# Last layer: context values and their sums from one product, the weights turned by transposes; feed-forward columns in fours, 64-row products side by side

## The chip, the core and the metric

The kernel runs on one core of one Trainium2 chip. The metric is the time of one execution on the device, in microseconds. The engines named below are TensorE (PE, with its weight loads shown as PEld), VectorE (DVE), ScalarE (ACT), GpSimd (POOL) and SyncE (SP), which issues most of the DMAs. Products accumulate in PSUM, which the kernel divides into eight banks of 128 x 512 fp32 values.

## What is computed

Four transformer layers over x of 8 batches x 256 tokens x 320 channels, with a context of 8 x 120 rows of 192 channels. Everything is fp32 but the attention of layer 0, which is quantised. In outline:

```python
# layer 0: quantised attention (20 heads of 16)
x = x + attention(ln(x), ln(x), Wq1, Wk1, Wv1, Wo1, bo1, 20)
x = x + attention(ln(x), ctx, Wq2, Wk2, Wv2, Wo2, bo2, 20)
x = x + (a * gelu(g)) @ W2 + b2        # a, g = split(ln(x) @ W1 + b1), 1280 each
# layer 1: the same without quantisation
# layer 2: attention to the first 104 context rows plus attention to the last 16, then Wo
# layer 3 (8 heads of 40): enc = ctx[:, :116], ca = ctx[:, 116:]
hs = mha(x @ Wq, enc @ Wk, enc @ Wv)
ca_q1 = einsum('btc,th->bch', ca, Wq_ca)[:, np.linspace(0, 191, 256).astype(int), :]
ca_hs1 = mha(ca_q1, x, x)
ca_hs2 = mha(ca_hs1 @ Wq, ca @ Wk_ca, ca @ Wv_ca)
out = (hs + ca_hs2) @ Wout + b_out + x
```

The 256 queries `ca_q1` of layer 3 are 192 distinct ones: the index list takes every third one twice.

## The kernel before

**Products.** 320 channels are two tiles of 128 rows and one of 64. So a projection is two "whole-row" products (K = 128) and one 64-row product. Where two outputs are made together, their 64-row operands lie on partitions 0–63 and 64–127, so that the two use different halves of PE's array. `duo` (L122) does this: whole rows of all outputs first, then the 64-row products of all. `by_weight` and `by_token` (L132–L140) list the three terms for weights or tokens as the stationary side. `mm` (L117) is a plain accumulation.

**PSUM.** The pool `ps_f` has three buffers of two banks (`pair()`), the pool `ps_a` two single banks (`bank()`). Whoever asks for a buffer waits until the older user of it has been read.

**Layer 0** is the class `Quant`. `project_all` (L1143) walks the eight batches: v of the batch (one `duo`), the turn of the next batch (`turned`: six transposes and four activations that apply the layer norm's scale and bias), q, k, and then the third column tile of q and k (`duo` each), and copies on ACT into SBUF. Scores, sums and outputs of self and cross attention follow; woven between them, `context_steps` (L642) makes keys and values of the context for layers 1, 2 and 3, stores them in DRAM (`kd`, `vd`), and `weights_last_steps` (L808) folds small weights of layer 3.

**Layers 1 to 3 and both feed-forwards** are a list of items that `run_flow` (L609) pipelines: 4 feed-forward blocks of 512 tokens, 8 self, 8 cross, 4 feed-forward blocks, 8 items of layer 2, 8 of layer 3. Each item has four parts (project, scores' maxima "tops", out, fin). At any time parts of up to four neighbouring items run, a step each in turn; a `yield` ends a step. The order so written is the order of the instructions on each engine, apart from what the tile scheduler moves.

A feed-forward block (`ff_item`, L545) makes ten column tiles i: a pair holds a_i and g_i; four whole-row products (L564), two 64-row products (L568), then ACT applies gelu to g_i (L572) and DVE multiplies (L573) into `hT`. The second product with `ff2` (L120) follows.

`load_last` runs after the last feed-forward: 40 DMAs for layer 2's `o`, 12 for `lwq`, 8 for `lwo` (`weight_heads3`, L783: the 40 rows of each head at rows 0–39 of a 64-row slot), then `open_last` (L793) with the folded weights, `sel` (192 x 256, one 1 per column: the repetition of every third query) and a tile of ones. They go through SP's queue, which also carries the rows of maxima (`qT<-nT`) from the scores of each head item into qT.

**A layer-3 item** (`last_item`, L878) works on one batch. Its out part makes scores of x as keys (`further`), their values with a second product of ones for the sums (`further_values`), scores of the context (`context`), the small softmax `p2` over four tokens, and four groups (two heads each) of `context_values` (L1043). The value tile `v` has 64 columns for each head, 40 values and 24 zeros. Each group makes two products with v into the left half of a bank and two with ones into the right half (all 64 rows of a head then hold the sum); DVE takes the reciprocal of the right half (L1054) and multiplies (L1055). At the end, `p2` (96 queries x 2 halves x 32) is turned and repeated by two products with `sel`, copied by ACT into `pT` (L1096), and `fin` (L1102) multiplies `oT` with `lwo` and `pT` with folded values. The tiles `rs`, `pT` and the gelu's `gl` share a tag with two buffers.

## Time and profile before

| | |
|---|---|
| median of 3 runs | 2272.55 us (2265.03 to 2274.88) |
| the profiled execution | 2260.05 us, span 2258.2 us |
| busy share of the span | PE 92%, PEld 52%, DVE 50%, ACT 37%, POOL 16% |
| chain that ended last | PE 74%, DVE 15%, ACT 4%, issue 2%, SP's queue 2% |
| stage (us from the start) | |
| layer 0: projections; self scores and sums; self out | 0–118; 118–274; 274–416 |
| layer 0: cross scores and sums; cross out | 416–545; 545–679 |
| feed-forward 0; layer-1 heads; feed-forward 1 | 679–990; 990–1453; 1453–1749 |
| layer-2 heads; layer 3 | 1749–1921; 1921–2258.2 |
| the feed-forward's L564: 640 passes; L568: 320 passes | 294.8 us; 90.3 us busy |
| layer-0 projections: time from batch to batch | 11.37 us |
| layer 3: time from item to item | 35.87 us |

"Busy" counts the time in which an engine executes; a PE that is busy can still be idle in part, since the profile gives each pass from its issue to its modelled end. The chain is followed back from the last instruction to whatever released each step. Stage borders are read from the times at which the first product of each kind starts. An fp32 product appears as two passes, so 640 passes of L564 are 320 products.

### The profile page before, as it was taken

The page shows a single profiled execution, that of the slowest core. Times are in us where ns is not written, and L with a number is a line of the kernel's source. Part 1 is how long each engine was busy: PE and PEld are TensorE (multiplying, and loading weights), DVE is VectorE, ACT ScalarE, POOL GpSimd, SP SyncE. Part 2 cuts the span into 40 slices and gives each one's busy share as a digit, 9 for nine tenths or more (in the row PEclk, how much of TensorE's full clock was granted, in tenths as well). Part 3 has the DMA queues.
Part 4 walks back from the last instruction along what each step waited for, and adds up shares of the span by engine and source line. Part 5 has one row for each costly group of instructions (what it writes and reads, how often), then busy time and mean ns, then how long its engine had stood idle before and what let it go on. Part 6 is the DMA issues. An engine that isn't in the chain of part 4 may idle for free.

```text
span 2258.2 us, 38244 instructions
## 1 busy us (share of the span) xinstructions
PE 2078.1 (92%) x16413; PEld 1177.0 (52%) x16413; DVE 1119.0 (50%) x1693; ACT 824.4 (37%) x1249; POOL 363.2 (16%) x368
## 2 busy tenths in 40 slices
PE   7978888898889999999999999899999799999997
PEld 4643345544444455465555555444455455566664
DVE  4288677444861221235555566611121566556465
ACT  2337878467542121124444443401201333222221
POOL 1093056620520000000000001100000100000100
PEclk9979889899899999999999999999999899999999
DMA  4010000542120000020000010100000201000000
GB/s 115 10 18 2 2 1 2 149 119 61 49 88 3 1 0 1 1 91 2 2 2 21 27 35 24 47 0 0 1 1 1 68 25 33 11 24 24 23 16 19
DMA packets 79304, 63.23 MB, mean 28 GB/s; under 512 B 48410, under 2 KB 68318, under 8 KB 78622
## 3 DMA queue, kind: packets, MB, share of 16 engines
q1 hardware_dynamic: 75070, 57.06, 9.0%
q10 hardware_dynamic: 4064, 3.71, 0.6%
q8 instruction: 130, 2.13, 0.4%
q14 instruction: 40, 0.33, 0.0%
HBM read 42.61 MB, written 17.37 MB: 27 GB/s over the span
## 4 chain that ended last, share of the span: by engine, by line
PE 74%; DVE 15%; ACT 4%; issue 2%; SPq 2%; DMA 1%; POOL 1%; ACTq 0%; DVEq 0%; POOLq 0%
PE pf L564 13%; PE pf L120 12%; PE pf L127 9%; PE pa L120 6%; PE pa L431 6%; PE pf L414 4%; PE pf L568 4%; PE pf L129 3%; DVE negm L1335 3%; PE pf L1376 3%; DVE rs L439 2%; PE pf L369 2%; PE pa L1398 2%; DVE negm L376 2%; DVE rs L1054 2%
## 5 line engine op out<-in xcount | busy, mean ns | idle before, releaser
L564 PE MATMUL pf<-xTf,ff 128*128 128x512 f32 x640 | 294.8, 603 | 3.5 <-DVE negm L376 2.5
L420 ACT ACTIVATE e<-pf 128x1024 f32<-128x1024 f32 (+2 forms) x176 | 157.7, 944 | 223.6 <-PE pf L414 216.8
L376 DVE TENSOR_REDUCE negm<-pf 128x4 f32<-128x1024 f32 (+4 forms) x224 | 187.8, 885 | 93.2 <-PE pf L369 93.2
L439 DVE RECIPROCAL rs<-pa 128x256 f32<-128x256 f32 x88 | 152.3, 1746 | 147.3 <-PE pa L431 147.3
L573 DVE SCALAR_TENSOR_TENSOR hT<-pf,cols_sb,gl 128x512 f32<-128x512 f32 x80 | 60.0, 750 | 331.2 <-ACT gl L572 331.2
L564 PEld LDWEIGHTS pf<-xTf,ff 128*128 128x128 f32 x640 | 115.1, 190 | 161.6 <-issue 154.9
L461 POOL TENSOR_TENSOR xb<-x_sb,brow 128x640 f32<-128x640 f32 x40 | 62.2, 1554 | 797.5 <-DVE x_sb L467 754.1
L1383 ACT ACTIVATE e<-pf,sc_s 128x1024 f32<-128x1024 f32 x160 | 169.6, 1117 | 50.8 <-PE pf L1376 44.7
L1335 DVE TENSOR_REDUCE negm<-pf 128x4 f32<-128x1024 f32 (+2 forms) x128 | 143.4, 1139 | 70.0 <-PE pf L1332 63.3
L120 PE MATMUL pf<-ff,hT 128*128 128x320 f32 x640 | 174.4, 434 | 0.0
L572 ACT ACTIVATE gl<-pf,cols_sb 128x512 f32<-128x512 f32 x80 | 55.0, 687 | 304.9 <-PE pf L568 304.9
L120 PEld LDWEIGHTS pf<-ff,hT 128*128 128x128 f32 x640 | 120.9, 190 | 55.5 <-issue 6.1
L414 PE MATMUL pf<-qT,kT 32*128 32x256 f32 (+1 forms) x1280 | 128.3, 411 | 19.3 <-DMA qT<-nT 11.0
L369 PE MATMUL pf<-kT,qT 32*128 32x120 f32 (+1 forms) x1920 | 112.7, 328 | 18.3 <-ACT e L420 18.3
L120 PE MATMUL pa<-o,oT 128*128 128x320 f32 x352 | 105.7, 442 | 12.8 <-DVE oT L440 11.6
L581 POOL TENSOR_TENSOR xb<-x_sb,brow 128x640 f32<-128x640 f32 x16 | 25.2, 1573 | 559.5 <-DVE x_sb L586 543.6
L369 PEld LDWEIGHTS pf<-kT,qT 32*128 32x128 f32 x1920 | 83.4, 189 | 55.4 <-ACT e L420 28.4
L1376 PE MATMUL pf<-Q,K 32*128 32x256 bf16 (+1 forms) x960 | 89.3, 294 | 24.9 <-DVE negm L1335 14.6
L431 PE MATMUL pa<-e,v 128*32 128x256 f32 (+1 forms) x1280 | 106.4, 389 | 2.3 <-ACT e L420 1.7
L414 PEld LDWEIGHTS pf<-qT,kT 32*128 32x128 f32 (+1 forms) x1280 | 72.2, 182 | 66.9 <-issue 34.6
L1491 DVE TENSOR_SCALAR w<-e 128x1024 bf16<-128x1024 f32 (+2 forms) x128 | 87.4, 691 | 37.4 <-ACT e L1383 36.4
L127 PE MATMUL pf<-xT,q 128*128 128x256 f32 x384 | 101.9, 394 | 2.1 <-DVE hT L573 1.9
(279 smaller groups left out, 3357.0 us busy)
## 6 DMA issues: line engine op xcount, KB each, us to landing
ff<-in_L_xattn_Wff_dram SPq DMA_DIRECT2D x1, 2560.0 KB
qT<-nT SPq DMA_DIRECT2D x160, 4.0 KB
ff<-in_L_xattn_ff_w_dram SPq DMA_DIRECT2D x1, 2560.0 KB
out_dram<-x_sb SPq DMA_DIRECT2D x16, 160.0 KB
kd_cross<-kst SPq DMA_DIRECT2D x8, 300.0 KB
vd_cross<-vst SPq DMA_DIRECT2D x8, 300.0 KB
vd_both<-vst SPq DMA_DIRECT2D x8, 300.0 KB
kT<-kd_cross SPq DMA_DIRECT2D x8, 300.0 KB
```

The costliest lines, as they stand in the source:

```text
L120: self.nc.tensor.matmul(out, l, r, start=i == 0, stop=i == len(pairs) - 1)
L127: self.nc.tensor.matmul(o, *t[c], start=c == 0, stop=False)
L369: nc.tensor.matmul(s[j // 2][:, j % 2, o : o + nk], qT[r : r + PAD, g, t * P : (t + 1) * P], kT[r : r + PAD, g, :nk], start=True, stop=True,)
L376: nc.vector.tensor_reduce(negm[:, n, 2 * i : 2 * i + 2, g0 : g0 + len(gs), :].rearrange("p j g t -> p j (g t)"), sv[:, :, :, k0:k1], AX.X, ...
L414: nc.tensor.matmul(s[j // 2][:ks, j % 2, o : o + N], kT[r : r + PAD, g, c * ks : (c + 1) * ks], qT[r : r + PAD, g, :], start=True, stop=True,)
L420: nc.scalar.activation(e[:ks, 2 * i : 2 * i + 2, :n], s[i][:ks, :, :n], AF.Exp, scale=scale)
L431: nc.tensor.matmul(o[j * PAD : (j + 1) * PAD, what * N : (what + 1) * N], w, es[g][:ks, j, c * N : (c + 1) * N], start=first and c == 0 an ...
L439: nc.vector.reciprocal(rs, o[:, N:])
L564: nc.tensor.matmul(s[:, k, :], w1[:, c, col : col + P], xT[:, c, :], start=c == 0, stop=False)
L1335: nc.vector.tensor_reduce(negm[:, 2 * h : 2 * h + 2, gs[0] : gs[-1] + 1, :].rearrange("p j g t -> p j (g t)"), s[:, :, : len(gs) * TPB * n ...
L1376: nc.tensor.matmul(s[at // 2][:ks, at % 2, o : o + N], l, m, start=not shift and o == 0, stop=shift and o + N == n, skip_group_check=True,)
L1383: nc.scalar.activation(e[:ks, :, :n], ps[:ks, :, :n], AF.Exp, scale=self.sc[:ks, 9:10])
```

## The change

It has six parts.

1. In a feed-forward block, column tiles go in fours: whole rows of tiles i and i+1, a step each; then the 64-row products of all four tiles; then whole rows of i+2 and i+3. The fourth tile lies in the two single banks. Tiles 8 and 9 form a rest of two. A manual dependency keeps the order of these products as it is written.
2. `duo` is split in `whole_rows` and `half_rows` with start and stop as arguments. `project_all` opens three pairs at once and issues v's whole rows, the 64-row products of v, q, k and their third tiles, the turn of the next batch, and then the whole rows of q, k and third tiles. The turn uses two single banks. The query projection of cross and layer-2 items, and the query and masked-key products of layer 3, are reordered likewise.
3. `both` in `context_steps` can start with the 64-row products, and `keys_to` uses this for the second column group.
4. The values of layer 3 are stored as 16 pieces of 20 values and 12 ones in place of 8 of 40 values and 24 zeros, and the weight `lwo` is placed to match, by 16 DMAs.
5. `context_values` makes the two products with v alone; lane 20 of each 32 is then the sum. DVE takes the reciprocal of all lanes, a stream shuffle copies lane 20 of each 32 to all 32, and the multiply follows. The ones tile goes.
6. `p2` is turned by two transposes, and three ACT copies write `pT` with every third query repeated. `sel` goes, with its DMA.

```diff
     def duo(self, outs, terms):
+        self.whole_rows(outs, terms, True, False)
+        self.half_rows(outs, terms, False, True)
+    def whole_rows(self, outs, terms, start, stop):
         n = len(terms[0]) - 1
         for c in range(n):
             for o, t in zip(outs, terms):
-                self.nc.tensor.matmul(o, *t[c], start=c == 0, stop=False)
+                self.nc.tensor.matmul(
+                    o, *t[c], start=start and c == 0, stop=stop and c == n - 1, skip_group_check=True
+                )
+    def half_rows(self, outs, terms, start, stop):
         for o, t in zip(outs, terms):
-            self.nc.tensor.matmul(o, *t[n], start=False, stop=True)
+            self.nc.tensor.matmul(o, *t[-1], start=start, stop=stop, skip_group_check=True)
...
-    def turned(self, x, dst, at, ln=None):
+    def turned(self, x, dst, at, ln=None, singles=False):
         nc = self.nc
-        ps = self.pair()
+        if singles:
+            ps = [self.bank(), self.bank()]
+        else:
+            pair = self.pair()
+            ps = [pair[:, 0, :], pair[:, 1, :]]
         for i, n in CH:
             for t in range(TPB):
                 o = i % 2 * N + t * P
-                nc.tensor.transpose(ps[:n, i // 2, o : o + P], x[:, t, i * P : i * P + n], self.ident)
+                nc.tensor.transpose(ps[i // 2][:n, o : o + P], x[:, t, i * P : i * P + n], self.ident)
...
             ps = self.pair()
-            self.duo([ps[:, m, :N] for m in range(2)], two((w["q"], w["q"]), (0, 1), 2))
-            yield
-            self.duo([ps[:, 0, N:]], two((w["q"],), (2,), 1))
+            outs, terms = [ps[:, m, :N] for m in range(2)], two((w["q"], w["q"]), (0, 1), 2)
+            last = [ps[:, 0, N:]], two((w["q"],), (2,), 1)
+            self.duo(outs, terms)
+            self.half_rows(*last, False, False)
+            yield
+            self.whole_rows(*last, False, True)
             self.put_q(qT, ps[:, :, :N], ps[:, 0, N:])
...
-                for k, col in ((1, (NF + i) * P), (0, i * P)):
+            s = {}
+            last = None
+            def mm(*args, **kw):
+                nonlocal last
+                ins = nc.tensor.matmul(*args, **kw)
+                if last is not None:
+                    order = mybir.DependencyInfo(mybir.DependencyClass.NoSync, mybir.DependencyReason.DATA)
+                    self.tc.add_manual_dep(ins.ins, last.name, order, reason="order of the rows' forms")
+                last = ins.ins
+            def whole(i, first):
+                for k in (1, 0):
                     for c in range(2):
-                        nc.tensor.matmul(s[:, k, :], w1[:, c, col : col + P], xT[:, c, :], start=c == 0, stop=False)
+                        col = (k * NF + i) * P
+                        mm(
+                            s[i][k], w1[:, c, col : col + P], xT[:, c, :], start=first and c == 0,
+                            stop=not first and c == 1,
+                        )
+            def halves(i, first):
                 for k in (1, 0):
                     r = 64 * k
-                    nc.tensor.matmul(
-                        s[:, k, :], w1c[r : r + 64, i * P : (i + 1) * P], xT[r : r + 64, 2, :], start=False, stop=True
+                    mm(
+                        s[i][k], w1c[r : r + 64, i * P : (i + 1) * P], xT[r : r + 64, 2, :], start=first,
+                        stop=not first,
                     )
+            def gated(i):
                 gl = self.work.tile([P, TB], F32, tag="gl", name="gl")
-                nc.scalar.activation(gl, s[:, 1, :], func, bias=self.cols[:, b1 + NF + i : b1 + NF + i + 1])
+                nc.scalar.activation(gl, s[i][1], func, bias=self.cols[:, b1 + NF + i : b1 + NF + i + 1])
                 nc.vector.scalar_tensor_tensor(
-                    hT[i // 4][:, i % 4, :], s[:, 0, :], self.cols[:, b1 + i : b1 + i + 1], gl, ALU.add, ALU.mult
+                    hT[i // 4][:, i % 4, :], s[i][0], self.cols[:, b1 + i : b1 + i + 1], gl, ALU.add, ALU.mult
                 )
-                yield
+            for i in range(0, NF, 4):
+                for j in range(i, min(i + 2, NF)):
+                    ps = self.pair()
+                    s[j] = ps[:, 0, :], ps[:, 1, :]
+                    whole(j, True)
+                    yield
+                for j in range(i, min(i + 2, NF)):
+                    halves(j, False)
+                    gated(j)
+                if i + 2 < NF:
+                    ps = self.pair()
+                    s[i + 2] = ps[:, 0, :], ps[:, 1, :]
+                    s[i + 3] = self.bank(), self.bank()
+                    for j in (i + 2, i + 3):
+                        halves(j, True)
+                    for j in (i + 2, i + 3):
+                        whole(j, False)
+                        gated(j)
+                        yield
...
-        def both(outs, whole, halves):
-            for i, o in enumerate(outs):
-                nc.tensor.matmul(o, *whole[i], start=True, stop=False)
-            for i, o in enumerate(outs):
-                nc.tensor.matmul(o, *halves[i], start=False, stop=True)
+        def both(outs, whole, halves, more=False):
+            for n, terms in enumerate((halves, whole) if more else (whole, halves)):
+                for i, o in enumerate(outs):
+                    nc.tensor.matmul(
+                        o, *terms[i], start=n == 0 and not more, stop=n == 1, skip_group_check=True
+                    )
...
-                st = self.vst[i][:, : H3 * PAD3].rearrange("p (h d) -> p h d", d=PAD3)
+                st = self.vst[i][:, : H3 * PAD3].rearrange("p (h d) -> p h d", d=PAD)
                 if b == 0:
-                    zero = self.ident[:, :1].unsqueeze(2).to_broadcast([P, H3, PAD3 - D3])
-                    nc.scalar.activation(st[:, :, D3:], zero, AF.Identity, scale=0.0)
-                nc.scalar.copy(st[:K3, :, :D3], ps[:K3, i, :C].rearrange("p (h d) -> p h d", d=D3))
-                nc.sync.dma_start(self.vd["last"][:K3, b + i], st[:K3])
+                    zero = self.ident[:, :1].unsqueeze(2).to_broadcast([P, 2 * H3, PAD - HALF3])
+                    nc.scalar.activation(st[:, :, HALF3:], zero, AF.Identity, scale=0.0, bias=1.0)
+                nc.scalar.copy(st[:K3, :, :HALF3], ps[:K3, i, :C].rearrange("p (h d) -> p h d", d=HALF3))
+                nc.sync.dma_start(self.vd["last"][:K3, b + i], self.vst[i][:K3, : H3 * PAD3])
...
         for h in range(H3):
-            r = h % 2 * PAD3
-            self.nc.sync.dma_start(w[r : r + D3, h // 2, :], src[h * D3 : (h + 1) * D3])
+            for i in range(2):
+                r, s = h % 2 * PAD3 + i * PAD, h * D3 + i * HALF3
+                self.nc.sync.dma_start(w[r : r + HALF3, h // 2, :], src[s : s + HALF3])
...
-        sel = w["sel"] = pool.tile([Q3, 2, N], F32, name="sel3")
-        nc.sync.dma_start(sel, self.a["sel"].rearrange("(t p) n -> p t n", p=Q3))
-        ones = w["ones"] = pool.tile([P, PAD3], F32, name="ones3")
-        nc.gpsimd.memset(ones, 1.0)
...
-            for r in range(2):
-                self.duo(
-                    [ps[:, i, r * N : (r + 1) * N] for i in range(2)],
-                    [self.by_weight(w["wq"], xT, 2 * r + i, i) for i in range(2)],
-                )
+            sums = [
+                ([ps[:, i, r * N : (r + 1) * N] for i in range(2)],
+                 [self.by_weight(w["wq"], xT, 2 * r + i, i) for i in range(2)])
+                for r in range(2)
+            ]
+            self.duo(*sums[0])
+            self.half_rows(*sums[1], False, False)
+            self.whole_rows(*sums[1], False, True)
...
-            for c, t in ((0, 0), (1, 0), (0, 1), (1, 1), (2, 0), (2, 1)):
+            for c, t in ((2, 0), (2, 1), (0, 0), (1, 0), (0, 1), (1, 1)):
...
             def context_values(g):
                 o = self.bank()
-                for what in range(2):
-                    for j in range(2):
-                        l = w["ones"][:K3] if what else v[:K3, 2 * g + j, :]
-                        nc.tensor.matmul(
-                            o[j * PAD3 : (j + 1) * PAD3, what * N : (what + 1) * N], l,
-                            es["c"][:K3, g // 2 * 2 + j, g % 2 * N : (g % 2 + 1) * N], start=what == 0,
-                            stop=what == 1, skip_group_check=True,
-                        )
+                for j in range(2):
+                    nc.tensor.matmul(
+                        o[j * PAD3 : (j + 1) * PAD3, :N], v[:K3, 2 * g + j, :],
+                        es["c"][:K3, g // 2 * 2 + j, g % 2 * N : (g % 2 + 1) * N], start=True, stop=True,
+                        skip_group_check=True,
+                    )
+                inv = self.work.tile([P, N], F32, tag="gl", name="inv")
+                nc.vector.reciprocal(inv, o[:, :N])
                 rs = self.work.tile([P, N], F32, tag="gl", name="rs")
-                nc.vector.reciprocal(rs, o[:, N:])
+                nc.vector.stream_shuffle(rs, inv, [HALF3] * PAD)
                 nc.vector.tensor_tensor(oT[:, g, :], o[:, :N], rs, ALU.mult)
...
             r = b * HT % P
             p2v = p2.rearrange("p (t h) k -> p t (h k)", t=2)
-            self.mm(ps[r : r + HT, :N], [(p2v[:, t, :], w["sel"][:, t, :]) for t in range(2)])
+            for t in range(2):
+                nc.tensor.transpose(ps[:HT, t * Q3 : (t + 1) * Q3], p2v[:, t, :], self.ident[:Q3, :Q3])
             pT = self.work.tile([P, N], F32, tag="gl", name="pT")
-            nc.scalar.copy(pT[r : r + HT], ps[r : r + HT, :N])
+            src = ps[:HT, :CC].rearrange("p (k i) -> p k i", i=3)
+            dst = pT[r : r + HT].rearrange("p (k i) -> p k i", i=4)
+            nc.scalar.copy(dst[:, :, 1:], src)
+            nc.scalar.copy(dst[:, 1:, 0], src[:, :-1, 2])
+            nc.scalar.copy(dst[:, 0, 0:1], src[:, 0, 0:1])
...
-            k.turned(x, xT, 0, self.ln)
+            k.turned(x, xT, 0, self.ln, True)
...
-            ps = k.pair()
-            k.duo([ps[:, t, :C] for t in range(TPB)], [k.by_token(w["v"], xT, t, t) for t in range(TPB)])
-            nc.scalar.copy(v, ps[:, :, :C])
+            pv, pq, pk = k.pair(), k.pair(), k.pair()
+            values = [pv[:, t, :C] for t in range(TPB)], [k.by_token(w["v"], xT, t, t) for t in range(TPB)]
+            qk = [
+                ([ps[:, m, :N] for m in range(2)], [k.by_weight(w[n], xT, m, m) for m in range(2)])
+                for ps, n in ((pq, "q"), (pk, "k"))
+            ]
+            last = [pq[:, 0, N:], pk[:, 1, N:]], [k.by_weight(w[n], xT, 2, i) for i, n in enumerate("qk")]
+            k.duo(*values)
+            for i in range(2):
+                k.half_rows(*qk[i], True, False)
+            k.half_rows(*last, False, False)
+            nc.scalar.copy(v, pv[:, :, :C])
             if b + 1 < B:
                 after = turn(b + 1)
+            for i in range(2):
+                k.whole_rows(*qk[i], False, True)
+            k.whole_rows(*last, False, True)
             qv, kv = (a.rearrange("p (c n) -> p c n", c=3) for a in (q, kt))
-            pq, pk = k.pair(), k.pair()
-            for ps, n in ((pq, "q"), (pk, "k")):
-                k.duo([ps[:, m, :N] for m in range(2)], [k.by_weight(w[n], xT, m, m) for m in range(2)])
-            k.duo([pq[:, 0, N:], pk[:, 1, N:]], [k.by_weight(w[n], xT, 2, i) for i, n in enumerate("qk")])
```

More of the change, by code (lines that the diff above doesn't have):

```diff
@@ L38 @@
 G3 = H3 * PAD3 // P
+HALF3 = D3 // 2
 T3 = 4
@@ L313, in turned @@
                 o = i % 2 * N + t * P
-                nc.tensor.transpose(ps[:n, i // 2, o : o + P], x[:, t, i * P : i * P + n], self.ident)
+                nc.tensor.transpose(ps[i // 2][:n, o : o + P], x[:, t, i * P : i * P + n], self.ident)
         if ln is None:
-            nc.scalar.copy(dst[:, :2, at : at + N], ps[:, 0, :].rearrange("p (c n) -> p c n", c=2))
+            nc.scalar.copy(dst[:, :2, at : at + N], ps[0].rearrange("p (c n) -> p c n", c=2))
             for r in (0, 64):
-                nc.scalar.copy(dst[r : r + 64, 2, at : at + N], ps[:64, 1, :N])
+                nc.scalar.copy(dst[r : r + 64, 2, at : at + N], ps[1][:64, :N])
             return
@@ L322, in turned @@
             nc.scalar.activation(
-                dst[r : r + n, i, at : at + N], ps[:n, i // 2, i % 2 * N : (i % 2 + 1) * N], AF.Identity,
+                dst[r : r + n, i, at : at + N], ps[i // 2][:n, i % 2 * N : (i % 2 + 1) * N], AF.Identity,
                 bias=self.cols[r : r + n, g + 3 : g + 4], scale=self.cols[r : r + n, g : g + 1],
@@ L559, in out @@
             hT = [self.hp.tile([P, 4, 512], F32, tag="big", name="hT", bufs=4) for _ in range(3)]
-            for i in range(NF):
-                s = self.pair()
-                for k, col in ((1, (NF + i) * P), (0, i * P)):
-                    for c in range(2):
-                        nc.tensor.matmul(s[:, k, :], w1[:, c, col : col + P], xT[:, c, :], start=c == 0, stop=False)
+            s = {}
[7 more added lines that the diff above has]
+                last = ins.ins
@@ L680, in keys_to @@
                     outs, [(w[:, 0, s], self.ctxT[:, 0, b, k0:k1]) for s in c],
-                    [(w[half(i), 1, s], self.ctxT[half(i), 1, b, k0:k1]) for i, s in enumerate(c)],
+                    [(w[half(i), 1, s], self.ctxT[half(i), 1, b, k0:k1]) for i, s in enumerate(c)], o > 0,
                 )
@@ L935, in project @@
                     ps[:, t, o : o + nh * HT], xT[rows, c, t * P : (t + 1) * P],
-                    bd[rows, c, :nh, :].rearrange("p h r -> p (h r)"), start=c == 0, stop=c == 2,
+                    bd[rows, c, :nh, :].rearrange("p h r -> p (h r)"), start=c == 2, stop=c == 1,
                     skip_group_check=True,
```

## The prediction

> **What bounds it now.** I read, in this order, the page's busy times and chain of waits, the windows by stage, and the timeline of TensorE (PE) inside one stage of each kind. PE is busy 92% of the span and carries 74% of the chain; VectorE (DVE) carries 15%. By stage (stretch; its us; busy us of PE, PE's weight loads, DVE, ACT, POOL; clock; DMA share; GB/s): the projections of layer 0, the two feed-forwards, and the last layer.
>
> ```profile
> 0.00:118.00 118.00, 94.74 (x434) 62.45 (x434) 41.87 (x104) 36.02 (x73) 14.27 (x37) 0.98 0.24 63
> 679.00:990.00 311.00, 307.12 (x1038) 152.78 (x1038) 68.39 (x120) 54.92 (x95) 17.98 (x22) 1.00 0.04 12
> 1453.00:1749.00 296.00, 294.01 (x984) 145.20 (x986) 51.20 (x78) 46.90 (x79) 13.28 (x10) 1.00 0.01 2
> 1921.00:2258.20 337.20, 312.45 (x2692) 200.58 (x2684) 186.90 (x233) 84.22 (x130) 23.39 (x33) 0.99 0.06 20
> ```
>
> The feed-forwards are PE's alone (98.8 and 99.3% busy, DVE at 22 and 17%), so what goes from PE there goes from the time. The projections are PE's from 30 us on. In the last layer PE is 93% busy and DVE 55%, in bunches: there a wait can take over.
>
> Inside a feed-forward block, PE's timeline (start, us, operation, passes; an fp32 product is two passes):
>
> ```profile
> 757.37 1.13 PE L568 MATMUL pf<-xTf,ff1c 64*128 64x512 f32 x4
> 758.43 3.70 PE L564 MATMUL pf<-xTf,ff 128*128 128x512 f32 x8
> 762.06 1.13 PE L568 MATMUL pf<-xTf,ff1c 64*128 64x512 f32 x4
> 763.12 2.41 PE L564 MATMUL pf<-xTf,ff 128*128 128x512 f32 x5
> ```
>
> Whole-row passes run one after another, 0.43 us apart, each with its weight load beside the pass before:
>
> ```profile
> 749.40 0.19 PEld L564 LDWEIGHTS pf<-xTf,ff 128*128 128x128 f32 x1 [0.24 <-issue]
> 749.83 0.19 PEld L564 LDWEIGHTS pf<-xTf,ff 128*128 128x128 f32 x1 [0.24 <-issue]
> ```
>
> Eight passes should take 3.43; from start to next group's start it is 762.06 − 758.43 = 3.63. Four 64-row passes run two at a time on the array's halves: 0.86, and it is 763.12 − 762.06 = 1.06. So **each switch between whole-row and 64-row products costs about 0.20 us**, of which some 0.09 is the array running empty and 0.10 a weight load that nothing covers (the two gaps in the same trace).
>
> **The change, part by part.** The compiled order of PE's instructions gives 1486 switches before, 1289 after: feed-forwards 196 to 86 (110 fewer), layer-0 self projections 65 to 18 (47 fewer), layer-1 heads 8 fewer, layer-2 heads 6, layer-0 cross attention and self output 13, last layer 13.
>
> 1. *Feed-forward, fours.* 110 × 0.20 = **−22.0**. One four used to pay 8 switches and pays 2. A run of eight 64-row products must keep its two-at-a-time pace; a steady run of 64-row pairs stands in the last layer:
>
> ```profile
> 2108.12 1.12 PE L1017 MATMUL pf<-qT,kz 64*116 64x256 f32 x8
> 2109.17 0.53 PE L1034 MATMUL pa<-ef,v 128*32 128x192 f32 x8
> ```
>
> Four pairs of 256 columns took 1.05 = 4 × 0.215 + 0.19, that is full pace and one switch. Here speaks a rule against the change: the Trainium skill, "TensorE: Matmul & The Clock Gate", Part 3, The mechanism, says that a weight load overlaps with products in flight only where its row group differs. By it, a longer run of whole-row products exposes each load, and of a switch only the 0.09 would be saved: −10 here. The trace decides against it for whole rows (loads at 0.43 us under passes of the same rows), so I take −22; −10 is the other end. PSUM cover: a pair is emptied by ACT (687 ns) and DVE (750 ns), about 1.8 us with the hand-over, and is asked for again at least two columns of whole rows (6.9 us) later: hidden. Only the fourth block of each feed-forward, woven with the next heads' score steps that use the same banks, has none to spare: PE waited 3.9 and 2.0 us there; **+1**, ends −1 and +4.
>
> 2. *Projections.* 47 × 0.20 = **−9.4** (ends −4.2 and −9.4). The transposes of the next batch come later, after all 64-row products; their four activations (2.04 us in the ACT timeline) still lie under 24 whole passes of 0.215 (5.2 us). The copies that empty q and k end 1.6 us after the last product (54.12 to 55.75), and the v product (3.1 us) comes before their banks' reuse. Once it costs: k's 64-row weights land near 25.0 us by their issue, and the first batch now asks for them about 1.1 us earlier: **+1.1**.
>
> 3. *Other switches.* Layer-1 heads run with PE 94% busy: 8 × 0.20 = −1.6. Layer 2 (PE 86%) and layer-0 attention (86–89%) have other waits that may take the place; half of 19 × 0.20: −1.9. **−3.5**, ends 0 and −5.4.
>
> 4. *SP's queue.* The last layer's weights are issued in one stretch after feed-forward 1, and behind them wait the rows that layer 2's first weighted scores need (SPq; start, us, operation, DMAs; then PE, with its wait):
>
> ```profile
> 1748.80 19.54 SPq L275 DMA_DIRECT2D o<-in_L_xattn_Wo_dram  x40
> 1768.44 9.58 SPq L776 DMA_DIRECT2D lwq<-in_L_xattn_Wq_rows_dram  x12
> 1778.13 3.10 SPq L790 DMA_DIRECT2D lwo<-in_L_xattn_Wout_dram  x8
> 1782.62 0.43 SPq L804 DMA_DIRECT2D sel<-in_sel_dram  x1
> 1783.15 6.13 SPq L397 DMA_DIRECT2D qT<-nT  x10
> 1788.55 2.19 PE L414 MATMUL pf<-qT,kT 32*120 32x256 f32 x16 [10.66 <-DMA qT<-nT]
> ```
>
> Eight more lwo DMAs are 3.1 us, sel goes (0.43): the wait grows by **+2.7** in full, as PE already stands still for it.
>
> 5. *Last layer.* Per item PE loses eight products with ones, which run in pairs (four times two passes of 0.215, 1.7), the sel product against two short transposes (about 0.65) and one or two switches (0.3): −2.7, over eight items −21. But the context values are where DVE is the chain:
>
> ```profile
> 2116.99 3.36 DVE L1054 RECIPROCAL rs<-pa 128x256 f32<-128x256 f32 x2
> 2120.27 0.69 DVE L1055 TENSOR_TENSOR oT<-pa,rs 128x256 f32<-128x256 f32 x2
> 2120.78 0.65 PE L1048 MATMUL pa<-ec,v 116*64 116x256 f32 x4 [0.72 <-DVE oT L1055]
> 2121.91 1.75 DVE L1054 RECIPROCAL rs<-pa 128x256 f32<-128x256 f32 x1
> 2123.57 1.06 DVE L956 TENSOR_REDUCE negm<-pf 128x8 f32<-128x928 f32 x1
> 2124.55 0.41 DVE L1055 TENSOR_TENSOR oT<-pa,rs 128x256 f32<-128x256 f32 x1
> ```
>
> DVE hardly rests, and PE stands for oT. The change puts one shuffle more between each reciprocal and product: four an item. Nearest row: the multiply of the same shape, 400 ns, so +1.6 us of DVE an item. The Trainium skill ("VectorE: DVE Perf Modes", The perf-mode tier table) has a shuffle at about 2400 ns for 2048 elements against 2293 for a tensor_tensor, so the same price; its Rules for kernel authors add that chained DVE operations should be few, which speaks against this part. By the order of instructions the fourth group's shuffle stands behind two maxima of the next item (about 1.2 each), the turned weights (three ACT copies for one) wait for a buffer that it frees, and the output product waits for them. Walking one item by these durations, PE's waits grow from 1.7 (L1048 behind oT and p, 13.2 over eight items) to about 4.5, against 2.7 less work: +0.2 an item, and 0.5 at the tail where nothing follows: **+2**. Ends: −10 (half of the saved work shows) and +12 (shuffle all on the chain, 32 × 0.4).
>
> The remaining edits cost nothing: the turn's two single banks instead of a pair (nothing else uses them in that stage), the other order of the masked-key products and of the context keys, and the fill with 1.0 where 0.0 was (the same instruction, the same bytes).
>
> Sum: −22.0 + 1.0 − 9.4 + 1.1 − 3.5 + 2.7 + 2.0 = **−28.1**. The profiled execution took 2260.05 (span 2258.2): 2232. The median of the runs, 2272.55 (2265.03 to 2274.88), lies 12.5 above it; I carry the difference over: **2244 us**.
>
> **The rivals.**
> - *The last layer pays.* The scheduler finds other PE work while DVE shuffles. For it: 93% busy PE and 21 us of products gone. Against: the wait for oT. Half the work shows: 12 lower, about **2232**.
> - *The switch price stays.* Longer runs save only the drain: feed-forward −10, projections −3, others −1.5, the rest as above +5.7: −9, **2264**. For: the rule of part 1 if it holds for mixed runs. Against: both steady runs shown.
> - *The other side: the four holds all eight banks.* Columns i to i+3 fill three pairs and two single banks. If emptying takes longer than the 6.9 us until reuse, PE stands at each of three groups in eight blocks for one emptying: 24 × 1.9 = +45, in all **2289**. For: there is no spare bank. Against: 1.8 us against 6.9, DVE at most 22% busy.
> - *The change doesn't do what it says.* The compiled order excludes it, but for the two woven blocks where runs are split.
>
> **How the numbers follow.** Forecast 0.65; last layer pays 0.15; price stays 0.12; banks 0.05; more waits in part 5 than its upper end together with the staying price 0.03. Differences under 0.5% (11.4 us) can't be told from none. The forecast's own range from its terms is 2232 to 2256. To 2226 below (last layer paying beside −28) and 2264 above it leaves about 2 in 10 out. Faster: 0.63 of the forecast, 0.15 of the second case and 0.05 of the third, whose own range straddles the limit: 0.83. Same: the 0.02 and 0.07 left of them: 0.09. Slower: 0.05 and 0.03: 0.08.
>
> **What would show it.** Right: in a feed-forward 64-row groups of 16 passes with 3.4 us + one switch between whole-row groups, and stages some 11 us shorter each; projection batches 10.2 us apart instead of 11.37; the wait for qT near 13; in the last layer PE's waits for DVE well above 13 us and its length about as now. Wrong: loads exposed inside 64-row runs, PE waiting for DVE in plain feed-forward blocks, or a shuffle far from 0.4 us.

## The result, and the profile after

| | before | after |
|---|---|---|
| median of 4 runs each | 2270.28 us (2265.03 to 2274.88) | 2248.9 us (2241.71 to 2250.4) |
| ratio | | 0.990, 95% interval 0.9868 to 0.9932 |
| the profiled execution, span | 2258.2 us | 2239.9 us |

The change saves 21.4 us of the 28.1 that were forecast (18.3 between the two profiled executions). By stage, from the first product of each kind in the two traces (length in us, and in brackets the time in it at half of TensorE's clock, added up from the records of the granted clock):

| stage | before | after | forecast | measured |
|---|---|---|---|---|
| layer-0 projections | 118.2 (5) | 108.9 (4) | −8.3 | −9.3 |
| layer-0 self, scores to output | 298.5 (57) | 297.0 (58) | about 0 | −1.5 |
| layer-0 cross | 262.0 (44) | 257.1 (41) | −1.3 | −4.9 |
| feed-forward 0 | 311.0 (0) | 301.6 (0) | −10.5 | −9.4 |
| layer-1 self and cross | 463.2 (3) | 468.9 (17) | −1.6 | +5.7 |
| feed-forward 1 | 296.8 (0) | 287.5 (0) | −10.5 | −9.3 |
| layer-2 heads | 171.8 (14) | 171.6 (17) | +2.1 | −0.2 |
| layer 3 | 336.7 (8) | 347.5 (63) | +2.0 | +10.8 |

The same in the windows of after (columns as before: stretch; us; busy us of PE, PE's loads, DVE, ACT, POOL; granted clock; DMA share; GB/s), for the projections, the two feed-forwards (the row of feed-forward 1 begins 8.8 us ahead of its first product) and the last layer:

```profile
0.00:108.90 108.90, 85.86 (x438) 66.52 (x442) 43.87 (x105) 36.01 (x73) 14.81 (x37) 0.98 0.26 69
663.00:964.50 301.50, 297.38 (x1036) 158.17 (x1036) 68.87 (x119) 54.88 (x95) 18.02 (x21) 1.00 0.04 12
1424.70:1720.84 296.14, 292.46 (x1112) 155.51 (x1100) 57.98 (x85) 51.22 (x86) 16.24 (x12) 1.00 0.01 3
1892.45:2239.91 347.46, 311.92 (x2530) 200.39 (x2528) 199.45 (x297) 84.96 (x145) 23.43 (x33) 0.91 0.06 19
```

The first three did nearly what was said. The last layer did not. Here it is in three stretches, of before and then of after: up to the first item's context values; five items, to the sixth one's; and from there to the end.

```profile
1921.51:2005.31 83.80, 80.43 (x711) 51.73 (x709) 43.50 (x49) 23.45 (x35) 7.04 (x10) 1.00 0.05 14
2005.31:2186.30 180.99, 172.44 (x1491) 113.26 (x1491) 99.89 (x125) 47.84 (x75) 13.29 (x21) 1.00 0.08 24
2186.30:2258.22 71.92, 59.07 (x475) 35.19 (x474) 43.44 (x59) 12.64 (x19) 3.07 (x2) 0.94 0.04 15
```

```profile
1892.45:1974.47 82.02, 78.64 (x712) 52.52 (x710) 43.51 (x49) 23.46 (x35) 7.03 (x10) 1.00 0.05 14
1974.47:2157.48 183.01, 169.58 (x1403) 112.21 (x1402) 107.62 (x165) 48.56 (x85) 13.29 (x21) 0.93 0.08 24
2157.48:2239.91 82.43, 63.70 (x421) 35.66 (x420) 48.32 (x83) 12.95 (x25) 3.11 (x2) 0.76 0.04 13
```

Over the layer PE is as busy in us as it was (311.94 then, 311.92 now) though it does 144 passes fewer, and its clock is 0.91 where it was 0.99: the work was taken away, and what remains runs slower. PE's idle time grew from 24.8 to 35.5 us, which is all of the +10.8. By place, the five items in the middle are 2.0 us longer and the last stretch 10.5.

Inside a feed-forward block of after, PE's timeline has the 64-row products of four column tiles, twelve passes into pairs and four into the single banks, as one run of 16 passes:

```profile
688.25 2.85 PE L583 MATMUL pf<-xTf,ff1c 64*128 64x512 f32 x12
690.93 1.02 PE L583 MATMUL pa<-xTf,ff1c 64*128 64x512 f32 x4
691.89 3.70 PE L583 MATMUL pf<-xTf,ff 128*128 128x512 f32 x8
```

691.89 − 688.25 = 3.64 us, eight times 0.43 and one switch of 0.20: full pace in the long run, no exposed loads.

SP's queue at the load of the last layer's weights, and PE's wait behind it (start, us, operation, count; the wait in square brackets):

```profile
1739.25 9.58 SPq L836 DMA_DIRECT2D lwq<-in_L_xattn_Wq_rows_dram  x12
1748.93 6.06 SPq L852 DMA_DIRECT2D lwo<-in_L_xattn_Wout_dram  x16
...
1756.45 5.85 SPq L412 DMA_DIRECT2D qT<-nT  x10
```

```profile
1761.32 1.22 PE L429 MATMUL pf<-qT,kT 32*120 32x256 f32 x8 [12.99 <-DMA qT<-nT]
```

The 16 DMAs take 6.06 us where eight took 3.10, and the wait is 12.99 where it was 10.66.

The last item of layer 3 on VectorE, one group of context values, and then PE's tail:

```profile
2220.56 1.75 DVE L1114 RECIPROCAL inv<-pa 128x256 f32<-128x256 f32 x1
2222.35 0.01 DVE L1116 LOAD_MASK_SELECT rs<-inv  x1
2222.35 0.43 DVE L1116 STREAM_SHUFFLE rs<-inv 128x256 f32<-128x256 f32 x1
2222.82 0.42 DVE L1117 TENSOR_TENSOR oT<-pa,rs 128x256 f32<-128x256 f32 x1
```

```profile
2223.39 0.48 PE L1157 MATMUL pa<-ident,p 96*32 96x96 f32 x2 [1.47 <-DVE oT L1117]
2226.00 4.64 PE L121 MATMUL pa<-lwo,oT 128*128 128x320 f32 x8 [2.13 <-ACT pT L1164]
...
2231.93 3.93 PE L121 MATMUL pa<-lwo,oT 128*128 128x320 f32 x8
```

The shuffle is 0.43 to 0.44 us, near the 0.40 of the multiply's row. Its mask load is 0.01. The eight passes of lwo take 4.64 and 3.93 us. In the tail of before the same two groups took 3.96 and 2.42:

```profile
2247.06 3.96 PE L120 MATMUL pa<-lwo,oT 128*128 128x320 f32 x8 [0.45 <-ACT pT L1096]
...
2251.68 2.42 PE L120 MATMUL pa<-lwo,oT 128*128 128x320 f32 x8
```

The long ones run at half clock, and no term of the forecast had that.

### The profile page after: what moved, and what is told of

Same layout as the page of the kernel before. It is cut to its first block, busy times and chain, and to the rows that moved or that the text cites. A ratio compares the mean times of both kernels' runs of the same rounds, so it can differ in the third digit from the quotient of the medians.

```text
span 2239.9 us, 38042 instructions
## 1 busy us (share of the span) xinstructions
PE 2044.5 (91%) x16269; PEld 1197.5 (53%) x16269; DVE 1132.3 (51%) x1757; ACT 824.2 (37%) x1265; POOL 363.5 (16%) x367
## 4 chain that ended last, share of the span: by engine, by line
PE 73%; DVE 16%; ACT 4%; issue 2%; SPq 2%; DMA 1%; POOL 1%; ACTq 0%; DVEq 0%; POOLq 0%
PE pf L583 13%; PE pf L121 12%; PE pf L133 9%; PE pa L121 6%; PE pa L446 6%; PE pf L429 4%; PE pa L583 3%; PE pf L140 3%; PE pf L384 3%; PE pf L727 3%; DVE negm L1412 3%; PE pf L1453 2%; DVE rs L454 2%; PE pa L1475 2%; DVE negm L391 2%
## 5 line engine op out<-in xcount | busy, mean ns | idle before, releaser
L583 PE MATMUL pf<-xTf,ff 128*128 128x512 f32 x512 | 230.8, 597 | 5.2 <-DVE negm L391 5.2
L610 DVE SCALAR_TENSOR_TENSOR hT<-pf,cols_sb,gl 128x512 f32<-128x512 f32 x64 | 48.0, 751 | 256.8 <-ACT gl L609 254.5
L583 PEld LDWEIGHTS pf<-xTf,ff 128*128 128x128 f32 x512 | 94.3, 190 | 124.3 <-issue 118.5
L609 ACT ACTIVATE gl<-pf,cols_sb 128x512 f32<-128x512 f32 x64 | 43.9, 687 | 247.9 <-PE pf L583 247.9
L384 PE MATMUL pf<-kT,qT 32*128 32x120 f32 (+1 forms) x1920 | 115.7, 331 | 18.6 <-ACT e L435 18.3
```

The costliest lines, as they stand in the source:

```text
L384: nc.tensor.matmul(s[j // 2][:, j % 2, o : o + nk], qT[r : r + PAD, g, t * P : (t + 1) * P], kT[r : r + PAD, g, :nk], start=True, stop=True,)
L583: ins = nc.tensor.matmul(*args, **kw)
```

## The experiments

Each kernel was timed in five rounds against the kernel before on the same chip; ratios are to that kernel. "Traced" is the one execution that the profile shows, with the lowest and the highest of that kernel's times: where it stands at an end of them, its stages need not be typical. "Layer 3" is the stage in that execution, with its half-clock time. The three kernels without the shuffle leave out the division by the sums.

| kernel | median, us | ratio (95%) | traced, us (lowest to highest) | layer 3, us (half clock) |
|---|---|---|---|---|
| the change again | 2244.55 | 0.9887 (0.9861–0.9914) | 2235.5 (2235.5–2250.6) | 345.0 (55) |
| fours alone | 2250.79 | 0.9911 (0.9882–0.994) | 2246.7 (2246.7–2258.7) | 337.1 (11) |
| old query order | 2248.03 | 0.9882 (0.9857–0.9907) | 2248.4 (2242.0–2249.7) | 344.5 (52) |
| parts 4, 5 and 6 undone | 2234.75 | 0.9826 (0.9799–0.9854) | 2236.1 (2226.0–2239.7) | 332.3 (11) |
| parts 4 and 5 undone | 2222.49 | 0.9789 (0.9761–0.9816) | 2228.8 (2212.3–2228.8) | 324.7 (10) |
| part 6 undone | 2247.46 | 0.9901 (0.9872–0.9929) | 2244.9 (2240.7–2253.0) | 346.9 (56) |
| ones kept, unread | 2248.11 | 0.9894 (0.9869–0.9919) | 2256.4 (2246.3–2256.4) | 356.3 (39) |
| ones kept in two groups | 2251.07 | 0.9907 (0.9874–0.994) | 2251.1 (2238.7–2257.7) | 352.5 (45) |
| no shuffle | 2234.97 | 0.9854 (0.9827–0.988) | 2245.5 (2231.8–2245.5) | 341.6 (56) |
| no shuffle, ones kept | 2226.07 | 0.9796 (0.9762–0.983) | 2229.5 (2214.2–2231.8) | 326.6 (15) |
| no shuffle, order forced | 2247.06 | 0.9902 (0.9872–0.9931) | 2243.1 (2239.2–2256.1) | 350.4 (56) |
| parts 4 and 5 undone, later loads | 2210.04 | 0.9753 (0.9725–0.9781) | 2207.7 (2207.7–2210.6) | 323.5 (8) |

**Fours alone** is the kernel before with the loop of `ff_item` replaced as in the change.

> The kernel before with the feed-forward in fours alone. Theory A (switches are worth 0.2 us each and nothing else in the stage changes): the two feed-forward stages are 9.4 us shorter each, as in the changed kernel; all other stages as before; 2270 - 18.8 = about 2251. Rival B (part of the 18.8 comes from neighbouring stages that moved with the rest of the change): 10 to 15 us in all, about 2257.

The feed-forwards are 303.3 and 288.3 us in its trace: 7.7 and 8.5 shorter, 16.2 in all, in an execution with 3.4 us of half clock in the first, which can have cost up to 1.7. The times' ratio makes 20 us, but its interval (14 to 27) does not tell the theories apart. By the stages it lies between the two, nearer to A; most of the fours' gain is its own.

**Old query order** undoes one part of the change:

```diff
-            self.duo(outs, terms)
-            self.half_rows(*last, False, False)
-            yield
-            self.whole_rows(*last, False, True)
+            self.duo([ps[:, m, :N] for m in range(2)], two((w["q"], w["q"]), (0, 1), 2))
+            yield
+            self.duo([ps[:, 0, N:]], two((w["q"],), (2,), 1))
```

> The changed kernel with the query projection of the cross and layer-2 items in its old order. In the changed kernel layer 1's heads took 5.7 us longer than before, with three spans of half clock (10 us) that were not there. Theory A (the earlier 64-row products bring TensorE sooner to its wait for the maxima, and that wait triggers the half clock): layer 1's cross part is 4 to 6 us shorter than in the changed kernel, about 2244; layer 2 loses 1 to 2 of that. Rival B (the dips depend on where the windows of the clock happen to fall): the same number of dips, no difference beyond 2 us.

Layer 1 is 464.8 us in this trace, against 468.9 in the change's. That looks like theory A, but **the change again**, with the change's own code, took 462.5:

> The changed kernel once more, unedited, as the control for the runs beside it: 2249 again. Layer 0's cross stage differed from 257 to 271 us in kernels with the same code for it, with 41 to 68 us of half clock in it; if that is chance, this run's cross stage need not be 257 again, while its last layer should again be near 347 us with about 60 us of half clock.

So theory A has no support: over the traces with that code, layer 1 takes 462.5 to 468.9 us, with 3 to 17 us of half clock, and layer 0's cross stage 257 to 271 with 37 to 68. In the change run again, layer 0's cross stage came out at 257.6, layer 3 at 345.0 with 55 us of half clock. Stages that wait differ by up to 14 us between executions of the same code. Layer 3 belongs to the change: 344.5 to 347.5 wherever its code is whole.

**Parts 4, 5 and 6 undone** puts the context values with their layout, the ones, sel and the eight lwo DMAs back, and keeps all else.

> The changed kernel with the context values, their layout, the ones, sel and its product as before (parts 4, 5 and 6 undone). Theory A (the last layer's shuffles and copies make TensorE wait, and the waits take its clock down to half): the last layer's stage goes back from 347 us to the 336.7 it had before, its granted clock from 0.91 to about 0.98, and the 2.1 us of the longer weight queue go too: some 12 us less than the changed kernel's 2249, about 2237. Rival B (the last layer grew for another reason than these parts, such as the order of its first products): no more than 3 us less.

Measured: 2234.75, and layer 3 at 332.3 with 11 us of half clock: theory A's case. Layer 3 is 4 us under that of the kernel before; of the change, only the order of its first products is left in that stage. Which part of the three loses?

**Parts 4 and 5 undone** puts the products with ones back, with the values and lwo laid out as before, and has this edit behind them; the weights are still turned by transposes:

```diff
...
-                nc.vector.reciprocal(inv, o[:, :N])
                 rs = self.work.tile([P, N], F32, tag="gl", name="rs")
-                nc.vector.stream_shuffle(rs, inv, [HALF3] * PAD)
+                nc.vector.reciprocal(rs, o[:, N:])
                 nc.vector.tensor_tensor(oT[:, g, :], o[:, :N], rs, ALU.mult)
```

**Part 6 undone** has the shuffles, and the product with sel:

```diff
-            for t in range(2):
-                nc.tensor.transpose(ps[:HT, t * Q3 : (t + 1) * Q3], p2v[:, t, :], self.ident[:Q3, :Q3])
+            self.mm(ps[r : r + HT, :N], [(p2v[:, t, :], w["sel"][:, t, :]) for t in range(2)])
...
```

> The changed kernel with the context values, their layout and the products with ones as before, but with the weights turned by transposes. If the shuffle is the loss: last layer 333 to 335 us, all but 1 or 2 us of what undoing all three parts gave (332.3), about 2237. If the transposes with their three copies are the loss: last layer near 345, about 2247.

> The changed kernel with the product with sel as before, but with the shuffled context values. If the shuffle is the loss: last layer 346 to 352 us (0.65 us more of product work an item), about 2250. If the transposes with their three copies are the loss: last layer about 335 us, 2238.

The shuffled values are the loss: 324.7 against 346.9 in layer 3. The transposes with their three copies gain 7.6 us (332.3 to 324.7) beside the old context values, and nothing that can be told beside the new ones (346.9 against 345.0 and 347.5).

**No shuffle** leaves out one instruction of VectorE in each group of context values:

```diff
-                rs = self.work.tile([P, N], F32, tag="gl", name="rs")
-                nc.vector.stream_shuffle(rs, inv, [HALF3] * PAD)
-                nc.vector.tensor_tensor(oT[:, g, :], o[:, :N], rs, ALU.mult)
+                nc.vector.tensor_tensor(oT[:, g, :], o[:, :N], inv, ALU.mult)
```

> The changed kernel without the shuffle: the context values are multiplied by each lane's own reciprocal, so the division by the sums is left out of the result. Theory A (the shuffle lies on the chain from one group of context values to the next and to the output product): 32 shuffles of 0.44 us and the gap before them, 14 to 15 us less in the last layer, and its half clock falls with the waits: 2232 to 2236. Rival B (it lies beside other work for most items, and the turned weights are what waits): 2 to 5 us less, about 2245.

The two measures disagree. The median is theory A's number, 10 us under the change run again. The traced execution is the longest of its six, and it is rival B's: layer 3 gained 3 to 6 us (341.6), and the half clock stayed at 56 us. So the shuffle's own price stays between 3 and 10 us. In this trace VectorE does what it does in the kernel with parts 4 and 5 undone, TensorE does 14 us less, and the stage is 17 us **longer** (the median 12.5). The windows of this trace, cut at the clock's own steps of 3.41 us, show what happens in each item (columns as above: PE's busy us come first after the length, the clock stands third from the end):

```profile
2099.01:2102.42 3.41, 3.08 (x34) 2.10 (x30) 3.41 (x8) 0.21 (x1) 0.00 (x0) 1.00 0.00 0
2102.42:2105.83 3.41, 1.71 (x16) 0.92 (x12) 3.41 (x5) 1.81 (x4) 0.00 (x0) 1.00 0.15 49
2105.83:2109.25 3.42, 3.42 (x10) 2.02 (x9) 2.06 (x2) 0.47 (x3) 0.00 (x0) 0.50 0.05 21
2109.25:2112.66 3.41, 3.41 (x13) 1.76 (x13) 0.00 (x0) 0.00 (x0) 0.00 (x0) 0.50 0.00 0
```

PE is idle for 1.70 us in the second window, and the next two run at half clock. Items then follow each other in 37.6 us, which is eleven of these windows: each item meets the clock's grid at the same place, and all fall into the same hole.

**Ones kept** (the change with the ones products in, unread), **ones kept in two groups**, and **no shuffle, ones kept** ask whether filling the hole brings the time back. In the first and the last the products are again the eight of an item before, while VectorE still reads the left half alone; in the second only for g > 1:

```diff
-                for j in range(2):
-                    nc.tensor.matmul(
-                        o[j * PAD3 : (j + 1) * PAD3, :N], v[:K3, 2 * g + j, :],
+                for what in range(2):
+                    for j in range(2):
+                        l = w["ones"][:K3] if what else v[:K3, 2 * g + j, :]
+                        nc.tensor.matmul(
+                            o[j * PAD3 : (j + 1) * PAD3, what * N : (what + 1) * N], l,
...
```

> The changed kernel with the 64 ones products kept beside it, their result unread. It adds 14 us of TensorE work in the last layer, in the places where it waits for VectorE. Theory A (waits take the clock down, the clock is most of the loss): the half-clock time in the last layer falls from 65 us towards the 10 it was, and the time does not rise: 2242 to 2249. Rival B (the VectorE chain alone sets the last layer, the clock costs nothing): the stage stays as it is within 2 us and half-clock time falls or not. Rival C (TensorE is the bound there): up to 14 us more, about 2262.

> The changed kernel, shuffles in, with ones products kept for the third and fourth group of context values alone, where TensorE's longest waits are: 7 us more work than the changed kernel. Theory A (as above): the idle in the fullest window of an item falls below 1.4 us only if these products lie in it; then half clock falls from 55 to 60 us to under 25 and the last layer from 345 to about 338, 2240. Rival B (the shuffles make the waits longer than the products can fill): half clock stays above 40 us, last layer 347 to 354, 2248 to 2254.

> The kernel without the shuffle (the division by the sums is left out of its result) with the 64 ones products kept, their result unread: VectorE's and ScalarE's instructions are those of the run without the shuffle, TensorE has 14 us more. Theory A (a stretch of one clock window, 3.4 us, with about 1.4 us or more of idle TensorE halves its clock for the next two windows, and the ones products fill that stretch): the last layer falls from 341.6 us to 325 to 328, its half clock from 56 to about 10 us, in spite of the added work; about 2224. Rival B (the order or the layout made the kernel with the ones brought back fast, not its filled waits): no fall; 342 or up to 14 more, 2235 to 2249.

With the shuffles in, filling does not pay: 14 us of products leave the median where it was (2248.11). In the trace, the longest of its six executions, they make layer 3 9 to 11 us longer, though half clock falls to 39 us; in two groups, 352.5 and 45. In the first the time is theory A's, but layer 3 is nearer to rival C; in the second, rival B. Without the shuffles theory A's numbers came, all but a half clock of 15 us in place of 10. The same kernel with and without 64 unread products, layer 3 in the windows, first with none and then with them:

```profile
1902.05:2243.68 341.63, 312.97 (x2530) 203.32 (x2528) 185.90 (x233) 84.98 (x145) 23.41 (x33) 0.92 0.06 19
```

```profile
1901.05:2227.70 326.65, 302.92 (x2658) 200.95 (x2656) 186.91 (x233) 85.05 (x145) 23.42 (x33) 0.98 0.07 20
```

128 passes more, 15 us less in the traces. By the medians it is 9 us, and the two ratios' intervals just overlap; the traced execution without the products is the longest of its six. But the kernel with parts 4 and 5 undone, which has as much work on both engines as the one with the products, is clear of it by its ratio (0.9789 against 0.9854). VectorE and ScalarE have the same instructions in both rows; the clock is 0.98. The first six items come 34.3 to 34.6 us apart, and no window is at half clock before the last item.

One doubt was left: the scheduler had also put the next item's first scores elsewhere in the two. **No shuffle, order forced** holds them back by a dependency, so that they stand behind the turn of the weights:

```diff
+                        if g == 0 and "turn" in w:
+                            order = mybir.DependencyInfo(mybir.DependencyClass.NoSync, mybir.DependencyReason.DATA)
+                            self.tc.add_manual_dep(ins.ins, w["turn"].name, order, reason="after the turn")
...
-                nc.tensor.transpose(ps[:HT, t * Q3 : (t + 1) * Q3], p2v[:, t, :], self.ident[:Q3, :Q3])
+                turn = nc.tensor.transpose(ps[:HT, t * Q3 : (t + 1) * Q3], p2v[:, t, :], self.ident[:Q3, :Q3])
+            w["turn"] = turn.ins
```

> The kernel without the shuffle (the division by the sums left out of its result), without ones products, with one order forced: the next item's first scores of x stay behind the turn of this item's weights, as they stand in the kernels with ones products; without that they stood ahead of it, and TensorE waited there for xT and ef, 1.7 us in one clock window. Theory A (the lost filling: with 1.7 us of products an item gone, a window of an item stays idle for 1.4 us wherever the scores stand): the last layer stays at 335 to 345 us with over 40 us of half clock, about 2235. Theory O (the order makes the wait, and the lost products only moved the order): no window of an item is idle for over 1.3 us, half clock under 20 us, and the last layer is at or under the 326 us of the kernel with ones, perhaps 315 to 325; 2215 to 2225.

Theory O falls. Layer 3 is 350.4 us with 56 at half clock, and the time 2247: theory A's side, but some 5 and 12 us beyond its numbers. The wait only moved, from the scores to the turn, and grew:

```profile
2091.01 0.65 PE L1110 MATMUL pa<-ec,v 116*64 116x256 f32 x4
2094.55 0.48 PE L1158 MATMUL pa<-ident,p 96*32 96x96 f32 x2 [2.89 <-DVE oT L1118]
```

TensorE waits there for VectorE's last multiply; with the ones in, its longest wait for VectorE at the context values and the turn is 0.72 us in the first six items.

**Later loads** is a version that uses both findings: parts 4 and 5 undone, and the load of the last layer's weights split, so that less stands in SP's queue ahead of the first maxima of layer 2.

```diff
-            w3["wq"] = k.weight_rows3(pool, "lwq", "L3_xattn_Wq_rows")
-            w3["wo"] = k.weight_heads3(pool, "lwo", "L3_xattn_Wout")
-            brow["last"] = k.bias_row(k.fk, 7)
-            k.open_last(pool, w3)
+            w3["pool"] = pool
+        def load_rows():
+            w3["wq"] = k.weight_rows3(w3["pool"], "lwq", "L3_xattn_Wq_rows")
+        def load_rest():
+            w3["wo"] = k.weight_heads3(w3["pool"], "lwo", "L3_xattn_Wout")
+            brow["last"] = k.bias_row(k.fk, 7)
+            k.open_last(w3["pool"], w3)
...
-        k.run_flow(items, before, {3: load_ff1, 12: load_ff1_row, 23: load_last})
+        k.run_flow(items, before, {3: load_ff1, 12: load_ff1_row, 23: load_last, 25: load_rows, 27: load_rest})
```

> The kernel with the ones brought back, and the last layer's weights loaded later: lwq two items into layer 2, lwo and the rest four items in, so that only layer 2's own 40 weight DMAs stand ahead of the first rows of maxima in SP's queue. Theory A (that queue is what TensorE waits for at the start of layer 2): the wait of 10 to 13 us for qT shrinks to nothing or a few us, layer 2 goes from 169 us to 156 to 160, and its 13.7 us of half clock, which follows the wait, to under 7: about 2212. Rival B (the later DMAs only move the wait to a later item's maxima): layer 2 stays above 165 us, 2219 to 2223.

```profile
1749.37 1.26 PE L429 MATMUL pf<-qT,kT 32*120 32x256 f32 x16 [3.27 <-DMA qT<-nT]
```

The wait is 3.27 us and layer 2 takes 161.1 us, against 169.0 with all loads in one stretch; its half clock is 6.8 us where it was 13.7. That is theory A, one us short of its range for the stage. By the ratio this kernel is 2.5% faster than the one before, the changed kernel 1.0%.

## Why the prediction was right, and where it was not

Direction and range held: 2248.9 against 2244, within 2226 to 2264. The forecast case is the one that came, but that the number is so near is in part luck: the profiled execution was forecast at 2232 and took 2241.7, nearly all of the difference in the last layer, and about half of it went again because the one of before lay 12.5 us under its median and the one of after 7.2.

- **The switch at 0.20 us held.** From block end to block end, the plain feed-forward blocks of after are 2.6 to 3.1 us shorter; 14 switches fewer are 2.8. Both feed-forwards gave −18.7 by the stage table against −21.0. The term that is short is that of the woven blocks, given as +1: the fourth blocks gained only 0.8 and 1.3 us, together 3.5 less than twice 2.8. PE waited there behind the heads' maxima (5.2 us in all at L583, against 2.5 before at L564).
- **The rule against the fours** (weight loads overlap only where the row group differs; the Trainium skill, "TensorE: Matmul & The Clock Gate", Part 3, The mechanism, which beside it names loads into a background weight buffer) would have given −10. The rows decided rightly: 16 passes of 64 rows took 3.64 us, and 15 whole-row passes in one run 6.60 (L583 at 1454.93), 0.43 from start to start.
- **Projections**: −9.3 against −8.3; a batch takes 10.17 us (51.05 to 61.22) where 10.2 was said.
- **SP's queue**: +2.3 at the wait itself (10.66 to 12.99) against +2.7. Eight DMAs fewer give layer 2 back 2.2 to 3.2 us (169.4 and 169.0 against 171.6 and 172.2).
- **Other switches**: −3.5 can't be checked. Layers 0 and 1 differ by more between two executions of the same code.
- **The last layer was mis-sized: +2.0 in the forecast, +10.8 measured (+8.3 when run again).** The shuffle's price (0.40) and the kind of the waits were right: VectorE has 12.6 us more work there, and waits appear at the turn of p and at the output product. The step that failed is the walk of one item "by these durations", with TensorE at full clock throughout. It took 2.7 us of work off each item, 21 in all; but PE's busy time in the layer did not fall (311.94 and 311.92 us), since the passes that remain ran longer. Its waits were to grow by 22 us, and PE's idle time grew by 10.8. Over the five items in the middle the two errors nearly cancel (+0.4 us an item against +0.2), which is luck: busy time fell by 2.9 us where some 13 were walked, idle time grew by 4.9 where 14 were. In the last stretch they don't cancel: three items at +0.2 and 0.5 for the tail were forecast, and it is 10.5 us longer (8.5 when run again), at a clock of 0.76 where it was 0.94.

  So a wait has a second price. Of the windows of 3.41 us with 1.4 us or more of idle time, 174 of 208 were followed by half clock (the last section counts them), for one to three windows, or longer if PE stays idle; the change's layer 3 has 63 us of that, before had 8. A us at half clock loses at most half a us, so 55 us more of it can cost 27. The 21 us that were taken from TensorE and the 10.8 that the stage grew are 32: 10.8 of it is idle time, and the rest is what the remaining passes take longer. How much of the idle time is the chain with the shuffles, and how much that chain's own slowing by the clock, these runs don't separate: the shuffle alone gave back 3 to 10 us and the products with ones alone none.
- **Rival 1** (the last layer pays) was wrong at the same place: 21 us of products went, and PE's busy time stayed. The rival of eight banks did not show: PE has no wait for a bank in the blocks that run alone. One of 0.70 us (at 1584.18, for the multiply at L610) stands in a block with the next heads' query projection between.

The profile of before had the clock in it: 0.99 in layer 3 and 0.87 in its last 31 us, where lwo's first eight passes took 3.96 us and the second eight 2.42. The forecast has no term for it, neither for a longer tail nor for longer waits in the items.

## What to carry to other kernels

Count TensorE's idle time by clock window before you take products away from a stage that waits for another engine: products beside a wait can be worth more than their own time, and here, without the shuffles, 64 useless ones made the stage 15 us shorter in the traces (9 by the medians); with the shuffles they gave nothing. Long runs of products of one tile form are a plain gain, at 0.2 us a switch. And if a change has several parts, time them apart: here the fours gained some 16 to 20 us, the projections 9 (by their stage alone), the transposes 7.6, and the shuffled values lost some 20.

## What the runs showed of the hardware

- **The clock follows idle time in windows of 3.41 us.** The records of the granted clock change only in steps of that length. Over twelve traces (before, after, and all in the table but the forced order and the later loads), with PE's idle time worked out for each window at full clock from 20 us on: of about 6400 windows with under 0.8 us idle, one was followed by half clock; of 534 with 0.8 to 1.4, 70; of 208 with more, 174. Back to full clock it went only after windows with under 0.6 us idle. The Trainium skill ("TensorE: Matmul & The Clock Gate", Part 1) tells of re-throttling after at least one idle window of about 3.4 us; here two fifths of a window was enough, and the measurement decides. Matmul ends are modelled in the trace, so the limit is rough.
- **An item's period can lock to these windows**: 37.6 us in the traced execution of the kernel without the shuffle, eleven windows, with the same 6.8 us of half clock in six items in a row.
- **The same code differs by half-clock time.** In the thirteen traces with the fours in, feed-forward 1, which has no half clock, took 287.5 us, or 288.3 in the two with the old query order, while layer 0's cross stage, which waits, took 257 to 271 us, longest where its half clock was longest (68 us). One set of eleven runs of the kernel before fell into 2264 to 2267 and 2275 to 2281, with nothing between. That the place of the windows decides this is likely, and was not tried.
